# The stores of q, h and the attention's result, and the transfers of the weight sums, from GpSimd's queue

## The chip, the cores and the metric

The kernel runs on one core of a Trainium2 chip, in fp32. The engines of the core work on their own instruction streams, each in order, and wait for each other by semaphores: TensorE (PE, with its weight loads PEld), VectorE (DVE), ScalarE (ACT), GpSimd (POOL) and SyncE (SP). A transfer between the chip's memory and SBUF is an instruction in the stream of the engine that issues it; what it needs must be there before it goes out, and what stands behind it on that engine waits as long. The metric is device time in microseconds, smaller is better, as the median of several runs.

## The reference

An AdaLN block: a modulated layer norm, a linear attention with 16 heads of 32, and a mixture of 8 experts of which each token takes two. B = 2 batches of N = 4096 tokens, C = 512 channels. Cut to what matters:

```python
x1 = layernorm(x) * (1 + scale1) + shift1          # scale, shift, gate from c @ wmod
q, k, v = x1 @ w_qkv.T                             # 16 heads of 32
q, k = relu(q), relu(k)
vk  = einsum('bhen,bhdn->bhed', [v, 1], k)         # sum over all tokens of a batch
att = einsum('bhed,bhdn->bhen', vk, q); att = att[:-1] / (att[-1] + EPS)
x = x + gate1 * (att @ w_proj.T + b_proj)
h = layernorm(x) * (1 + scale2) + shift2
p, idx = top_k(softmax(rms(h) @ router_logits), 2)
for e in range(8):                                 # each token with its two experts
    g = h @ gating[e]                              # two halves, 512 wide each
    y[e] = (gelu(g[0]) * g[1]) @ linear[e]
out = x + gate2 * sum over the two experts of p * y
```

## The kernel before

**Blocks and passes.** The tokens are cut into 16 blocks of 512 (`TB`), eight a batch, each of four tiles of 128. vk is a sum over a whole batch, so each batch is passed twice. The first pass (`first`) makes k and q of each block, adds k^T x to a sum (L795), and writes q to the chip's memory (`q_d`). The second pass (`merge`, `attend`, `second_norm`, `route`) reads q again, makes the attention's result, adds it to x and writes that to `out`, makes the normalised h and writes it to `h2_d` (`h_d` in the profile's rows), and sends for each token and expert a small record to the map `map_d` (16 scatters a block, L1153, on POOL). The expert stage then gathers h's rows and each unit's expert weights by index (L1421 is the helper that issues the gathers, on POOL) and adds its results into `out` by scatters (L1488, POOL).

**Order of the work.** A planner weaves these parts, and a scheduler fixes each engine's order before the run. In the profile: the first pass of batch 0 to about 396 us, then the first pass of batch 1 between the second passes of batch 0 to about 876 us, then the second passes of batch 1 between the first nine large expert units to about 1410 us, then the rest of the expert units.

**Seven products for eight.** k and q of a block are made by seven quarter products in place of eight, in the order 1, 2, 6, 7, 5, 4, 3. Products 1, 2 and 4 take quarters of the turned block `xT` as they are; 6, 7, 5 and 3 take sums of quarters. `turned_sums` (L679 to L682) makes these on POOL, four operations a block, into `xs`. In batch 0 `xs` has one buffer, so a block's sums can't begin before PE's last product of the block before; in batch 1 it has two and is made a block ahead. The expert products have the same form, and need sums of quarters of the weights: `weight_sums` (L584 to L621) makes them during the first pass of batch 0, as 24 jobs (two gate halves and one linear matrix for each of eight experts). A job loads 1 MB into a buffer `wraw` (tag `tmp`, two buffers for all of them), makes four sums in place on POOL (L617), and stores 1 MB to `wgsum_d` or `wlsum_d` (L618). Three jobs are drawn for each block. The loads (L598) and stores are SP's; a job's load is issued right behind the store of the job two ahead of it, which had the same buffer, and the first two stand in front of all.

**The stores.** q is written in four stores of 256 KB a block (L777), each right behind ACT's relu of that tile (L774), from ACT's queue; q has four tiles of buffer. ACT also makes k's relu there, and PE's k^T x (`pa`, L795) takes k. The attention's result (L974, `out<-xb`) and h (L1007, `h_d<-h`) are each written in one store of 1 MB a block, also from ACT's queue.

Of the kernel before, what the change touches and what calls it, by code (L numbers as in the profile page):

```python
# [17 lines left out]
P = 128  # L18
B, N, C = 2, 4096, 512
# [34 lines left out]
def adaln_linear_attention_moe_kernel(  # L54
# [27 lines left out]
    nc = tc.nc  # L82
# [17 lines left out]
        out=upper, in_=ones, compare_op=ALU.is_gt, fill=0.0, base=0,  # L100
# [5 lines left out]
        out=head_mask, in_=ones[:, 0:GH], compare_op=ALU.is_ge, fill=0.0, base=0,  # L106
# [3 lines left out]
        out=head_mask, in_=head_mask, compare_op=ALU.is_ge, fill=0.0, base=HD - 1,  # L110
# [53 lines left out]
    def row(tag, name, bufs, where=bk):  # L164
        return where.tile([P, C], FP, tag=tag, name=name, bufs=bufs)
# [72 lines left out]
    raw = {}  # L238
# [345 lines left out]
    def weight_sums():  # L584


        jobs = []
        for e in range(E):
            rows = slice(e * P, (e + 1) * P)
            for m in range(2):  # L590
                src = wgate[rows, m * 4 * KH * QN : (m + 1) * 4 * KH * QN]
                r0 = (2 * e + m) * P
                jobs.append((src, wgsum_d[r0 : r0 + P, :], True))
            jobs.append((wlin[rows, :], wlsum_d[rows, :], False))

        def load(n):
            raw = temp(f"wraw_{n}")
            nc.sync.dma_start(out=raw.rearrange("p q n -> p (q n)"), in_=jobs[n][0])  # L598
            return raw

        ready = [load(0), load(1)]
        yield
        for n, (_, dst, left) in enumerate(jobs):
            raw = ready.pop(0)
            a, b, c, d = (raw[:, q, :] for q in range(4))
            if left:
                steps = (
                    (c, d, c, ALU.add), (d, a, d, ALU.subtract),
                    (a, c, a, ALU.subtract), (b, b, a, ALU.subtract),
                )  # L610
            else:
                steps = (
                    (a, d, a, ALU.subtract), (d, c, d, ALU.subtract),
                    (c, c, a, ALU.subtract), (b, b, c, ALU.subtract),
                )
            for to, one, two, op in steps:
                nc.gpsimd.tensor_tensor(to, one, two, op)  # L617
            nc.sync.dma_start(out=dst, in_=raw.rearrange("p q n -> p (q n)"))  # L618
            if n + 2 < len(jobs):
                ready.append(load(n + 2))  # L620
            yield  # L621


    q_d = dram.tile([B * NBLK * P, NT * C], FP, tag="qd", name="q_d")
# [60 lines left out]
    def first(b, i, acc, ksum):  # L685
# [15 lines left out]
        def lane(m, c):  # L701

            one, two = banks_of(m, c)
            at = E if m else 0
            top, low = slice(0, QN), slice(QN, C)
            for t in (c, c + 2):
                if m:
                    out_of[m][t] = row("qo", f"q_{b}_{i}_{t}", 4, ap)
                else:
                    out_of[m][t] = row("k", f"k_{b}_{i}_{t}", 4, ap)  # L710
            upper_t, lower_t = out_of[m][c], out_of[m][c + 2]

            def product(s, to):
                f = forms[m, s]
                a = at - (AHEAD.get(s, 0) if m else 0)
                for k in range(KH):
                    nc.tensor.matmul(
                        to[:, a : a + f.shape[2]], xs[s][:, k, c * P : (c + 1) * P],
                        f[:, k, :],
                        start=(k == 0 and s in (1, 2, 7)), stop=(k == KH - 1 and s in (2, 4, 3)),  # L720

                        skip_group_check=True,
                    )

            def keep(t, cols, src, new):

                to = out_of[m][t][:, cols]
                nc.vector.scalar_tensor_tensor(
                    to, src[:, at : at + QN], mv[:, t, 1:2],
                    bias[m, b][:, cols] if new else to, ALU.mult, ALU.add,  # L730
                )

            def logits(t, src, c0, new):
                to = xl[:, tile0 + t, 0:E]
                if new:
                    nc.vector.tensor_copy(to, src[:, c0 : c0 + E])
                else:
                    nc.vector.tensor_tensor(to, src[:, c0 : c0 + E], to, ALU.add)

            behind = at + QN  # L740
            for s in ORDER:
                to = two if s in (2, 7, 4) else one
                product(s, to)
                if s == 1:
                    keep(c, top, to, True)
                    if m:
                        logits(c, to, 0, True)
                elif s == 2:
                    keep(c, top, to, False)
                    if m:  # L750
                        logits(c, to, behind, False)
                elif s == 6:
                    keep(c + 2, top, to, True)
                elif s == 7:
                    keep(c + 2, low, to, True)
                elif s == 5:
                    keep(c + 2, low, to, False)
                    if m:
                        logits(c + 2, to, behind, True)
                elif s == 4:  # L760
                    keep(c + 2, top, to, False)
                    if m:
                        logits(c + 2, to, behind, False)
                else:
                    keep(c, low, to, True)
                yield
            for t in (c + 2, c):
                r = out_of[m][t]
                if m == 0:
                    if i == 0 and c == 0 and t == 2:  # L770
                        nc.vector.tensor_scalar(ksum, r, 0.0, None, ALU.max)
                    else:
                        nc.vector.scalar_tensor_tensor(ksum, r, 0.0, ksum, ALU.max, ALU.add)
                nc.scalar.activation(r, r, AF.Relu)  # L774
                if m:
                    r0 = (b * NBLK + i) * P
                    nc.scalar.dma_start(out=q_d[r0 : r0 + P, t * C : (t + 1) * C], in_=r)  # L777

        for lanes in (
            ((0, 0), (0, 1)), ((1, 0), (1, 1))  # L780
# [115 lines left out]
    def attend(b, i, kall, gm):  # L896

        r0 = b * N + i * TB
# [65 lines left out]
        for step in range(NT + 2):  # L964
            if step < NT:
                weigh(step)
            if 1 <= step <= NT:
                turn(step - 1)
            if step >= 2:
                project(step - 2)  # L970
            if step == NT and i + 1 < NBLK:
                load_xb(b, i + 1)
            if step == NT + 1:
                nc.scalar.dma_start(  # L974
                    out=out[r0 : r0 + TB, :].rearrange("(p t) c -> p t c", t=NT), in_=xt
                )
            yield

    def second_norm(b, i):

        xt = xatt.pop((b, i))
        r0 = b * N + i * TB
        blk = b * NBLK + i
        group = group_of[blk]
        lm, var, ssq = tokens[group[0]]
        j0 = (blk - group[0]) * NT
        at = slice(j0, j0 + NT)
        nc.scalar.activation(var[:, at], var[:, at], AF.Sqrt, bias=eps_ln, scale=1.0 / C)
        nc.vector.reciprocal(var[:, at], var[:, at])
        h2 = temp(f"h2_{b}_{i}", 0)  # L990
        for step in range(NT + 2):
            if step < NT:
                j = j0 + step
                nc.vector.scalar_tensor_tensor(
                    h2[:, step, :], xt[:, step, :], lm[:, j, E : E + 1], batch_rows[CB],
                    ALU.add, ALU.mult,
                )
                nc.vector.scalar_tensor_tensor(
                    h2[:, step, :], h2[:, step, :], var[:, j : j + 1], batch_rows[SB],
                    ALU.mult, ALU.add,  # L1000
                )
                sq = row("sq", f"sq_{b}_{i}_{step}", 1)
                nc.scalar.activation(
                    sq, h2[:, step, :], AF.Square, accum_out=ssq[:, j : j + 1]
                )
            if step == NT:
                nc.scalar.dma_start(  # L1007
                    out=h2_d[r0 : r0 + TB, :].rearrange("(p t) c -> p t c", t=NT), in_=h2
                )
                if b + 1 < B and i == NBLK - 1:  # L1010
                    for n in (SB, CB):
                        batch_row(n, b + 1)
            if step == NT + 1 and blk == group[-1]:
                route(b, group, *tokens.pop(group[0]))
            yield
# [873 lines left out]
```

## Time and profile before

| what | value |
|---|---|
| median of 3 runs | 2304.97 us (2301.86 to 2310.61) |
| the profiled execution | 2372.11 us |
| its span, mean granted clock of PE | 2370.4 us, 0.981 |
| transferred, mean rate over the span | 513.29 MB, 217 GB/s |
| POOL's queue, both others (share of 16 DMA engines) | 40.1%, 20.4% and 5.5% |

The profiled execution took 67 us longer than the median of the runs. Rows of the profile name the line, the engine, the operation, the tile written and read, the count, then the busy time in us, the mean duration of one in ns, and the idle time of the engine just ahead of such instructions with what ended most of it. Timeline rows begin with the start in us and the duration; "SPq" and "ACTq" are transfer issues in SP's and ACT's queue; what stands in brackets is the idle time ahead and what ended it. "Clock" is the share of full speed that PE was granted.

### The profile page before, as it was taken

The page shows a single profiled execution, that of the slowest core. Times are in us where ns is not written, and L with a number is a line of the kernel's source. Part 1 is how long each engine was busy: PE and PEld are TensorE (multiplying, and loading weights), DVE is VectorE, ACT ScalarE, POOL GpSimd, SP SyncE. Part 2 cuts the span into 40 slices and gives each one's busy share as a digit, 9 for nine tenths or more (in the row PEclk, how much of TensorE's full clock was granted, in tenths as well). Part 3 has the DMA queues.
Part 4 walks back from the last instruction along what each step waited for, and adds up shares of the span by engine and source line. Part 5 has one row for each costly group of instructions (what it writes and reads, how often), then busy time and mean ns, then how long its engine had stood idle before and what let it go on. Part 6 is the DMA issues. An engine that isn't in the chain of part 4 may idle for free. (4 is left out here: it accounts for less than half of the span.)

```text
span 2370.4 us, 26081 instructions
## 1 busy us (share of the span) xinstructions
PE 2257.7 (95%) x9456; PEld 1702.1 (72%) x9456; DVE 1523.0 (64%) x3251; ACT 535.0 (23%) x976; POOL 963.2 (41%) x840
## 2 busy tenths in 40 slices
PE   8999989999988999989998889999999999999997
PEld 4576657777766758878887767777777777777775
DVE  4866647786977756767876765555555555555554
ACT  1121212232323302333333411111111111111110
POOL 1266663003223242343535356444444444544432
PEclk9999999999999999999999989999999999999999
DMA  7688886444544444647684557777777777777774
GB/s 271 244 310 324 333 313 230 166 152 138 178 164 110 127 160 166 215 152 239 171 256 150 162 169 241 250 249 247 249 250 250 235 237 248 244 249 256 245 222 89
DMA packets 120189, 513.29 MB, mean 217 GB/s; under 512 B 19365, under 2 KB 22181, under 8 KB 84090
## 3 DMA queue, kind: packets, MB, share of 16 engines
q0 software_dynamic: 64704, 296.79, 40.1%
q1 hardware_dynamic: 41530, 164.45, 20.4%
q10 hardware_dynamic: 13824, 50.34, 5.5%
q8 instruction: 77, 1.26, 0.2%
q14 instruction: 54, 0.44, 0.1%
HBM read 378.97 MB, written 132.55 MB: 216 GB/s over the span
## 5 line engine op out<-in xcount | busy, mean ns | idle before, releaser
L1512 PE MATMUL p_g<-xT,wg 128*128 128x256 f32 x1600 | 373.0, 380 | 0.0
L1512 PEld LDWEIGHTS p_g<-xT,wg 128*128 128x128 f32 x1600 | 303.4, 191 | 45.7 <-issue 5.2
L1512 PE MATMUL p_g<-xS,wg 128*128 128x256 f32 x1200 | 286.6, 381 | 14.9 <-DVE quar_l L1520 7.6
L1512 PEld LDWEIGHTS p_g<-xS,wg 128*128 128x128 f32 x1200 | 227.4, 191 | 51.2 <-issue 8.1
L946 PE MATMUL po<-gm,qT 128*128 128x265 f32 (+1 forms) x1024 | 247.2, 391 | 4.6 <-issue 2.6
L795 PE MATMUL pa<-k,xh 128*128 128x512 f32 x512 | 234.2, 611 | 16.4 <-ACT k L774 16.3
L946 PEld LDWEIGHTS po<-gm,qT 128*128 128x128 f32 x1024 | 194.3, 194 | 40.2 <-issue 5.5
L1488 POOL DMA_INDIRECT out<-y_b,mp x100 | 162.7, 1627 | 129.2 <-DVE y_b L1485 101.2
L1153 POOL DMA_INDIRECT map_d<-pair,slot x128 | 133.5, 1043 | 176.0 <-DVE slot L1150 138.4
L1705 PE MATMUL pgs<-wgs,xTs 128*128 128x512 f32 x464 | 203.9, 592 | 0.0
L1512 PE MATMUL p_l<-wl,aT 128*128 128x256 f32 x800 | 193.7, 380 | 2.6 <-DVE part_l L1520 2.6
L795 PEld LDWEIGHTS pa<-k,xh 128*128 128x128 f32 x512 | 99.0, 196 | 134.4 <-issue 108.1
L617 POOL TENSOR_TENSOR wraw<-wraw 128x512 f32<-128x512 f32 x96 | 135.7, 1417 | 88.9 <-DMA wraw<-in_wgate 36.0
L1705 PEld LDWEIGHTS pgs<-wgs,xTs 128*128 128x128 f32 x464 | 88.2, 190 | 110.5 <-issue 109.5
L1512 PEld LDWEIGHTS p_l<-wl,aT 128*128 128x128 f32 x800 | 148.8, 191 | 23.6 <-DVE part_l L1520 3.0
L1512 PE MATMUL p_l<-wl,aS 128*128 128x256 f32 x600 | 144.0, 383 | 0.6 <-DVE aS L1622 0.6
L679 POOL TENSOR_TENSOR xs<-xT 128x512 f32<-128x512 f32 x16 | 21.3, 1330 | 292.1 <-DMA xT<-in_xturned 173.1
L1520 DVE TENSOR_TENSOR quar_g<-part_g,p_g 128x512 f32<-128x512 f32 x150 | 102.5, 684 | 51.1 <-PE p_g L1512 46.5
L1611 ACT ACTIVATE ge<-quar_g 128x512 f32<-128x512 f32 x100 | 63.0, 630 | 312.2 <-DVE quar_g L1520 300.9
L1512 PEld LDWEIGHTS p_l<-wl,aS 128*128 128x128 f32 x600 | 114.3, 192 | 17.9 <-issue 1.4
L1421 POOL DMA_INDIRECT xg_b<-h_d,mp x100 | 100.9, 1009 | 64.1 <-issue 32.5
L1520 DVE TENSOR_TENSOR part_g<-part_g,p_g 128x512 f32<-128x512 f32 x100 | 68.5, 686 | 83.8 <-PE p_g L1512 78.8
(343 smaller groups left out, 3734.7 us busy)
## 6 DMA issues: line engine op xcount, KB each, us to landing
xT<-in_xturned SPq DMA_DIRECT2D x16, 1024.0 KB
x<-in_x SPq DMA_DIRECT2D x16, 1024.0 KB
q_d<-q ACTq DMA_DIRECT2D x64, 256.0 KB
xb_d<-x SPq DMA_DIRECT2D x16, 1024.0 KB
qi<-q_d SPq DMA_DIRECT2D x64, 256.0 KB
wraw<-in_wgate SPq DMA_DIRECT2D x16, 1024.0 KB
wgsum_d<-wraw SPq DMA_DIRECT2D x16, 1024.0 KB
xb<-xb_d SPq DMA_DIRECT2D x16, 1024.0 KB
```

What stands on the lines that cost most here:

```text
L617: nc.gpsimd.tensor_tensor(to, one, two, op)
L679: nc.gpsimd.tensor_tensor(s7, x00, x10, ALU.subtract)
L795: nc.tensor.matmul(pa, xh[t][:, g * P : (g + 1) * P], ks[t], start=(t == 0), stop=(t == NT - 1),)
L946: nc.tensor.matmul(po[:, C // 2 - EX + c0 : C // 2 - EX + c1], qT[:, g * P : (g + 1) * P], gm[:, g, c0:c1], start=(g == 0), stop=(g == KC ...
L1153: ins = nc.gpsimd.indirect_dma_start(out=map_d, out_offset=IndirectOffsetOnAxis(ap=slot[:, k, t : t + 1], axis=0), in_=pair[:, k, t, :], i ...
L1421: return nc.gpsimd.indirect_dma_start(out=dst, out_offset=None, in_=src, in_offset=IndirectOffsetOnAxis(ap=ids, axis=0))
L1488: ins = nc.gpsimd.indirect_dma_start(out=out[0:N, :] if early else out, out_offset=IndirectOffsetOnAxis(ap=token(mp, t), axis=0), in_=y, i ...
L1512: nc.tensor.matmul(bank[:, c, :], left(s, c, k), rhs[:, k, :], start=(k == 0), stop=(k == KH - 1),)
L1520: nc.vector.tensor_tensor(r, one, two, ALU.add)
L1611: nc.scalar.activation(ge, g, AF.Gelu_apprx_tanh)
L1705: nc.tensor.matmul(p, xT[:, k, :], wg[:, :, quarters[k // KH], k % KH, :], start=(k == 0), stop=(k == KC - 1),)
```

## The change

In `weight_sums` loads and stores go out from GpSimd's queue. Only the first load stands in front; the load for job n+1 is written just ahead of the sums of job n, and the load behind the store is gone. The stores of q, of the attention's result and of h go out from GpSimd's queue too. That is 144 transfers (24 loads, 24 stores of sums, 64 of q, 16 of the result, 16 of h); their sizes, buffers and the sums themselves are as before. Where an instruction stands in POOL's final order is the scheduler's choice.

```diff
 def load(n):
     raw = temp(f"wraw_{n}")
-    nc.sync.dma_start(out=raw.rearrange("p q n -> p (q n)"), in_=jobs[n][0])
+    nc.gpsimd.dma_start(out=raw.rearrange("p q n -> p (q n)"), in_=jobs[n][0])
     return raw

-ready = [load(0), load(1)]
+ready = [load(0)]
 yield
 for n, (_, dst, left) in enumerate(jobs):
+
+    if n + 1 < len(jobs):
+        ready.append(load(n + 1))
     raw = ready.pop(0)
...
     for to, one, two, op in steps:
         nc.gpsimd.tensor_tensor(to, one, two, op)
-    nc.sync.dma_start(out=dst, in_=raw.rearrange("p q n -> p (q n)"))
-    if n + 2 < len(jobs):
-        ready.append(load(n + 2))
+    nc.gpsimd.dma_start(out=dst, in_=raw.rearrange("p q n -> p (q n)"))
     yield
...
-                    nc.scalar.dma_start(out=q_d[r0 : r0 + P, t * C : (t + 1) * C], in_=r)
+                    nc.gpsimd.dma_start(out=q_d[r0 : r0 + P, t * C : (t + 1) * C], in_=r)
...
-                nc.scalar.dma_start(
+                nc.gpsimd.dma_start(
                     out=out[r0 : r0 + TB, :].rearrange("(p t) c -> p t c", t=NT), in_=xt
                 )
...
-                nc.scalar.dma_start(
+                nc.gpsimd.dma_start(
                     out=h2_d[r0 : r0 + TB, :].rearrange("(p t) c -> p t c", t=NT), in_=h2
                 )
```

## The prediction

> **What bounds the kernel now.** I read the busy table first, then the same figures cut by stage, then the engines' timelines around the moved instructions.
>
> ```profile
> PE 2257.7 (95%) x9456; PEld 1702.1 (72%) x9456; DVE 1523.0 (64%) x3251; ACT 535.0 (23%) x976; POOL 963.2 (41%) x840
> ...
> L617 POOL TENSOR_TENSOR wraw<-wraw 128x512 f32<-128x512 f32 x96 | 135.7, 1417 | 88.9 <-DMA wraw<-in_wgate 36.0
> L1153 POOL DMA_INDIRECT map_d<-pair,slot x128 | 133.5, 1043 | 176.0 <-DVE slot L1150 138.4
> ```
>
> PE has work for 95% of the span, so the change can give only what PE now waits, and can take as much as it makes PE wait. POOL's 41% is a mean; by stages (window, length, then PE, PEld, DVE, ACT, POOL busy with counts, clock, DMA share, GB/s) it is not even:
>
> ```profile
> 106.00:396.00 290.00, 275.35 (x1011) 191.22 (x1010) 181.50 (x403) 56.21 (x91) 174.80 (x128) 0.98 0.85 318
> 396.00:876.00 480.00, 457.06 (x1876) 341.08 (x1875) 364.52 (x942) 142.80 (x287) 121.91 (x109) 0.98 0.44 141
> 1410.00:2371.00 961.00, 945.47 (x3912) 701.38 (x3911) 520.39 (x864) 150.30 (x263) 436.84 (x380) 0.99 0.75 236
> ```
>
> From 106 to 396 us, batch 0's first pass, POOL is busy 60% and the DMA engines 85%, at 318 GB/s. Here POOL makes both the weight sums (L617) and the sums xs of each turned block (L679 to L682), which PE needs 3.5 us after a block's start. From 1410 us on nothing the change touches is left. The timelines show the two places where a moved instruction holds PE now:
>
> ```profile
> 331.90 0.61 ACT L774 ACTIVATE q<-q 128x512 f32<-128x512 f32 x1
> 339.43 0.34 ACTq L777 DMA_DIRECT2D q_d<-q  x1
> 339.81 0.63 ACT L774 ACTIVATE k<-k 128x512 f32<-128x512 f32 x1 [7.29 <-DMA wlsum_d<-wraw]
> ...
> 340.49 15.10 PE L795 MATMUL pa<-k,xh 128*128 128x512 f32 x28 [6.87 <-ACT k L774]
> ...
> 768.48 3.78 PE L795 MATMUL pa<-k,xh 128*128 128x512 f32 x4 [8.39 <-ACT k L774]
> ```
>
> ACT has q ready at 332.5 but its store is not issued until 339.4 (it waits for a transfer), the next relu of k stands behind it, and PE behind that. At 758 to 766 us the same happens.
>
> **What the change takes away.** 96 issues leave ACT (64 of q, 16 of the result, 16 of h) and 48 leave SP. At 0.33 us that is 32 us of ACT, which is 77% idle: nothing by itself. By the Trainium skill ("DMA: Bandwidth & Descriptors", section "Issuing engines are not separate DMA queues") another issuing engine saves only the time to start a transfer, so the gain would be 0. The rows above weigh against it: the wait at the issue is the price. The first stall costs PE 6.87 us, and the 28 products after it took 15.10 us where 28 took 12.28 us at 213.7 us, 2.8 more: 9.7 us. The second costs 8.39 us and 14 products after it took 8.44 us, against 6.1 at that pace: 10.7 us. I take both as gone, **−20.4 us**; what is late next at these places is DVE's q (3.7 us of ACT's wait at 757.5), already inside PE's pace. Other waits of PE of this kind sum to under 1 us.
>
> SP's queue gets free of `SPq L618 <- POOL wraw` (115 us) and of the loads' waits behind it (37 us). SP then issues x and xT earlier. Their issue costs no PE wait now, so: nothing.
>
> **What it adds on POOL in batch 0.** Each of the 24 jobs before had its load two ahead on SP. These rows show one:
>
> ```profile
> 175.15 0.33 SPq L618 DMA_DIRECT2D wlsum_d<-wraw  x1
> 179.87 0.33 SPq L598 DMA_DIRECT2D wraw<-in_wgate  x1
> ...
> 180.34 1.27 POOL L679 TENSOR_TENSOR xs<-xT 128x512 f32<-128x512 f32 x1
> ...
> 186.87 5.31 POOL L617 TENSOR_TENSOR wraw<-wraw 128x512 f32<-128x512 f32 x4 [1.23 <-DMA wraw<-in_wgate]
> ```
>
> The store at 175.15 has landed 4.7 us later, when the load into the same buffer goes out; it lands 7.0 us after its issue, while POOL makes a block's xs. In the changed kernel there are still two buffers, so load n+1 waits for store n−1, and it stands in POOL's own order among job n's instructions. The scheduler's static order of the changed kernel puts it on average after 2.94 of job n's four sums' worth of work (47 over 16 jobs). Job n+1's sums then wait for it to land. So a job takes a load's latency plus what stands ahead of the next load; nothing of POOL's own is between except the xs steps.
>
> Latency: 7.0 us under load, 5.0 us with little in flight (358.64 to 363.64 us), plus 0.6 for POOL's own issue (0.95 us against SP's 0.33): 5.6 to 7.6 us, **taken 6.6**, as this stage is at 85% of the DMA engines. Sums: 5.31/4 and a gap each, 1.38 us. A job: 6.6 + 2.94 × 1.38 = **10.7 us**. It took 10.2 before (16.3 jobs from xs of block 2 at 132.70 to xs of block 6 at 298.27 us), but that had xs and all else inside.
>
> Between the same two points the new order has 16.7 jobs: 178 us; xs steps not under a load, about 8 × 1.38 = 11; q stores ahead of loads, about 8 × 1.26 = 10 (an indirect DMA on POOL is 1.04 us and its gap 0.2). Sum 199 us, against four blocks of 39.7 us, 159. So POOL falls **40 us** behind PE, where it had 2 to 7 us in hand before. Walking down POOL's order block by block with these prices, xs is late by 12 us at block 3, 17 at block 4 (five jobs before it), 2 at block 5 and 8 at block 6; then the jobs are used up. That is 39. Inside xs itself the third sum (L681) stands behind the first sum of a job whose load was just issued, so the latency stands inside PE's wait. The same walk with latency 5.5 gives 26 us, with 7 gives 44 and with 8 gives 56.
>
> **What hides the rest.**
> - The q stores wait on ACT's relu and block POOL behind them. In batch 0 that is in the walk; in batch 1 xs is a block ahead (slack 65 to 85 us). q's four buffers are free 28 to 40 us before reuse; the 16 map scatters ahead of some stores take 16 × 1.27 = 20 us. Hidden; without that cover up to 10 us a block.
> - The stores of the result and of h: their tiles have 30 to 40 us. In the stage from 876 to 1410 us 16 to 20 of them add 20 us to a POOL with 213 us of work in 534. One store of h stands ahead of a gather of wg, which goes some 12 us later with 30 in hand. At the stage's start four q stores stand before the gathers of xg: 2.5 us with 5 to 8 in hand. Taken as 0, bound 0 to 15.
> - 144 issues themselves: 0.95 to 1.27 us each. The Trainium skill ("SBUF — State Buffer", section "A bandwidth-pool intuition that's wrong (but worth ruling out)") speaks against the change: a transfer from GpSimd's queue took about 620 ns alone but about 3100 beside a copy on DVE, as the descriptors wait for a shared port. By the rule 144 × 2.5 = 360 us of POOL, and 30 us more in the walk's 12 or so exposed issues. The trace: 128 scatters into map_d, beside a DVE busy 76% of that stage, mean 1043 ns. I go by the row.
>
> **Sum.** 39 − 20.4 = +19 us. On the profiled execution, 2372.1 us, 2391 us. The median shown is 67 us (2.9%) below that execution; the waits are transfers and do not scale with it, so 2305 + 19 = **2324 us**.
>
> **Rivals.**
> 1. *Faster: the ACT stalls outweigh.* Place: the loads of wraw in batch 0. Price: the latency of one; below 5.0 us PE's loss falls under the 20.4 us gained (the walk gives 22 us at 5.0, 16 at 4.0), and a queue of SP's that waits for nothing could remove part of the other waits: PE idles 14.7 us from 106 to 396, of which I counted 6.9, and 22.9 from 396 to 876, of which 8.4. Half of the rest is 11. For it: 5.0 us at 358 us, and the median is 67 us shorter than this execution. Against: that load had the queues to itself. 16 − 20.4 − 11 = −15, 2290; with less of it, 2300.
> 2. *Nothing measurable.* Latency near 5.5 and one stall returning elsewhere: +26 − 20 = +6, 2300 to 2316. For it: DMA share 0.85 is high, not full. Against: five jobs stand ahead of block 4's xs whatever the latency.
> 3. *POOL is much worse.* Issues at 1.63 us (the row of the scatters out<-y_b), latency 8 or more, a gather of weights held behind a store: 56 + 12 × 0.7 + 15 − 20 = +59, 2364. For it: 318 GB/s already, and a store and a load now contend from one queue. Against: SP's transfers leave the other queue empty.
>
> That the change does not do what it says is out: the order shows 144 issues on POOL and none of these on ACT or SP.
>
> **Chances.** Likeliest case (+12 to +40) 0.50, rival 1 0.15, rival 2 0.23, rival 3 0.12. About 0.5% (11.5 us) is what a measurement of this kernel can tell from no change, so faster is below 2293, slower above 2316.5. Two thirds of rival 1 lie below, the rest and all of rival 2 between: faster 0.10, same 0.28, slower 0.62. The likeliest case's own range is 2315 to 2345; the range with a part of rivals 2 and 3 is 2297 to 2360.
>
> **What would show it.** Right: PE waits of 10 us or so before the product with xs at blocks 3, 4 and 6 of batch 0, released by POOL's last two steps of xs; POOL waiting for the load of wraw 6 to 7 us a job; the two waits at `pa <- k` gone; the end of batch 0's pass at about 396 + 29 us. Wrong: POOL's waits for wraw under 4 us, PE's blocks still 39.7 us long in batch 0; PE waits in the stage after 876 us released by POOL's gathers; POOL's new issues over 2 us each beside DVE.

## The result: 2.4% slower, and the profile after

| | us |
|---|---|
| changed kernel, median of 4 runs | 2362.0 (2356.3 to 2365.3) |
| kernel before beside it, median of 4 runs | 2303.4 (2300.5 to 2310.6) |
| ratio, 95% interval | 1.0247 (1.0215 to 1.0279) |
| forecast | 2324, range 2297 to 2360 |

The loss is 58 us, three times the 19 that were forecast. Here is the page of the changed kernel (the busy times and three of its groups: busy us and mean ns, then the idle time ahead and what ended it):

```profile
PE 2250.7 (96%) x9456; PEld 1706.3 (72%) x9456; DVE 1523.9 (65%) x3251; ACT 533.9 (23%) x975; POOL 1037.5 (44%) x984
...
L796 PE MATMUL pa<-k,xh 128*128 128x512 f32 x512 | 227.6, 598 | 0.3 <-ACT k L775 0.3
...
L620 POOL TENSOR_TENSOR wraw<-wraw 128x512 f32<-128x512 f32 x96 | 131.5, 1371 | 90.4 <-DMA wraw<-in_wgate 43.8
...
L778 POOL DMA_DIRECT2D q_d<-q x64 | 35.6, 557 | 235.4 <-ACT q L775 235.4
```

The busy shares of the engines tell little: PE even has a larger one. What is to be seen is in the idle columns. PE's wait for ACT's k is gone (0.3 us), a plain transfer costs POOL 0.56 us, and POOL now stands for 235 us at stores of q (none of it in the first pass of batch 0). The list of waits of the same kernel (us in total, times, longest) has what is new:

```profile
DVE h L995 <- DMA h_d<-h: 45.9, 6, 15.3
POOL wraw L620 <- DMA wraw<-in_wgate: 43.8, 15, 8.4
POOL wraw L620 <- DMA wraw<-in_wlin: 43.0, 8, 8.5
...
PE p0one L718 <- POOL xs L682: 35.9, 5, 13.6
```

POOL waits for the landing of nearly every load of weights, 3.8 us each, and PE waits 35.9 us for POOL's xs, which it did not do before. The longest of these waits, in POOL's timeline (start, duration) and then in PE's:

```profile
246.02 0.56 POOL L598 DMA_DIRECT2D wraw<-in_wlin  x1
...
248.36 0.54 POOL L621 DMA_DIRECT2D wgsum_d<-wraw  x1
252.50 1.26 POOL L620 TENSOR_TENSOR wraw<-wraw 128x512 f32<-128x512 f32 x1 [3.59 <-DMA wraw<-in_wlin]
253.72 1.25 POOL L680 TENSOR_TENSOR xs<-xT 128x512 f32<-128x512 f32 x1
...
258.58 0.56 POOL L598 DMA_DIRECT2D wraw<-in_wgate  x1
...
260.38 1.26 POOL L682 TENSOR_TENSOR xs<-xT 128x512 f32<-128x512 f32 x1
```

```profile
247.05 1.05 PE L718 MATMUL p1two<-q,xT 128*128 128x264 f32 x4
261.70 2.08 PE L718 MATMUL p0one<-k,xs 128*128 128x256 f32 x4 [13.59 <-POOL xs L682]
...
267.19 1.03 PE L718 MATMUL p0one<-k,xT 128*128 128x256 f32 x4
```

xs of this block can't start until a sum in front of it has its load, and that load was issued only at 246.02. When PE goes on, its first four products take 2.08 us instead of 1.03.

### The profile page after: what moved, and what is told of

Same layout as the page of the kernel before. It is cut to its first block, busy times and chain, and to the rows that moved or that the text cites. A ratio compares the mean times of both kernels' runs of the same rounds, so it can differ in the third digit from the quotient of the medians.

```text
span 2354.5 us, 26084 instructions
## 1 busy us (share of the span) xinstructions
PE 2250.7 (96%) x9456; PEld 1706.3 (72%) x9456; DVE 1523.9 (65%) x3251; ACT 533.9 (23%) x975; POOL 1037.5 (44%) x984
## 5 line engine op out<-in xcount | busy, mean ns | idle before, releaser
L1513 PEld LDWEIGHTS p_g<-xS,wg 128*128 128x128 f32 x1200 | 228.9, 192 | 39.9 <-issue 4.3
L947 PE MATMUL po<-gm,qT 128*128 128x265 f32 (+1 forms) x1024 | 239.8, 383 | 1.0 <-ACT qT L939 0.7
L796 PE MATMUL pa<-k,xh 128*128 128x512 f32 x512 | 227.6, 598 | 0.3 <-ACT k L775 0.3
L1513 PEld LDWEIGHTS p_l<-wl,aT 128*128 128x128 f32 x800 | 149.0, 191 | 20.4 <-issue 2.2
L778 POOL DMA_DIRECT2D q_d<-q x64 | 35.6, 557 | 235.4 <-ACT q L775 235.4
L1714 DVE TENSOR_TENSOR ar<-pgs,ges 128x512 f32<-128x512 f32 x29 | 20.1, 692 | 150.7 <-PE pgs L1706 145.3
```

Of the source, the lines that this page charges most:

```text
L778: nc.gpsimd.dma_start(out=q_d[r0 : r0 + P, t * C : (t + 1) * C], in_=r)
L796: nc.tensor.matmul(pa, xh[t][:, g * P : (g + 1) * P], ks[t], start=(t == 0), stop=(t == NT - 1),)
L947: nc.tensor.matmul(po[:, C // 2 - EX + c0 : C // 2 - EX + c1], qT[:, g * P : (g + 1) * P], gm[:, g, c0:c1], start=(g == 0), stop=(g == KC ...
L1513: nc.tensor.matmul(bank[:, c, :], left(s, c, k), rhs[:, k, :], start=(k == 0), stop=(k == KH - 1),)
```

## The experiments

Chips differ: the kernel before had a median of 2305 us on the chips of e9 to e15, 2356 on that of e1 to e4 and 2377 on that of e5 to e8. So each ratio is to runs of before on the same chip, and profiles are set side by side where their chips' times of before agree; where they don't, the text says so. The length of a block in the first pass of batch 0, below, is from one end of its last product `pa` to the next.

**e1, the kernel before once more.** No edit. The profile that the forecast read took 67 us longer than the median, so the first question was whether its waits are to be had at all.

> The kernel before, unchanged, profiled a second time: the profile that the prediction used took 67 us longer than the median. Theory A (the two waits of ACT at q's store, 6.9 and 8.4 us of PE, belonged to that one execution): this profile is near 2305 us, PE has no gap over 4 us at pa behind ACT's k, the first pass of batch 0 ends near 386 us. Theory B (they are in every execution): both gaps are here again, the pass ends near 396 us.

This execution took 2363.7 us, on a chip where that is normal (2356.4). The pass ended at 388.7 us, and PE's waits at pa were:

```profile
PE pa L795 <- issue: 4.0, 1, 4.0
PE pa L795 <- ACT k L774: 3.5, 7, 1.4
```

3.5 us behind ACT's k in place of 16.3; the gap of 6.87 us is not there, and what is left of the other is 4.0. On the two gaps theory A holds; its time near 2305 us did not come, and need not on this chip. The stages tell where the 67 us of the forecast's profile lie. From the last `pa` of batch 0 to that of batch 1 it took 479.9 us, e1 473.8 and e10 (below, a chip at 2305) 450.2; from there to the last product `po` of batch 1, 454.2, 460.1 and 421.7. So 62 us of its distance to e10 lie in these two stages, and it runs there like a chip such as e1's; the two gaps are a small part. On which chip it ran is not on record.

**e2, e3 and e4, parts of the change alone.**

```diff
 # e2: as the change, but
-    nc.gpsimd.dma_start(out=q_d ...)   # and out, h2_d
+    nc.scalar.dma_start(out=q_d ...)
 # e3: as before, but
-    nc.scalar.dma_start(out=q_d ...)   # and out, h2_d
+    nc.gpsimd.dma_start(out=q_d ...)
 # e4: as before, but
-    nc.sync.dma_start(out=dst, in_=raw ...)
+    nc.gpsimd.dma_start(out=dst, in_=raw ...)
```

> Only the weight sums' loads and stores go from GpSimd's queue, as in the change; q, the result and h stay on ACT. Theory A (the loads wait in POOL's own order and make xs late): the four PE gaps before the products with xs stay, the first pass loses about 40 us, time about 2345. Theory C (the q stores in POOL's order hold the sums): the gaps go, time under 2320.

> Only the stores of q, of the result and of h go from GpSimd's queue; the weight sums stay on SP as before. Theory A: no PE gap at xs over 3 us, time 2303 to 2320, the part above 2303 being what the change costs outside the first pass. Theory C: over 2335.

> Only the stores of the weight sums go from GpSimd's queue; the loads stay on SP two ahead. The bytes on GpSimd's queue are half those of the change's sums. Theory A (what costs is that POOL itself waits for a load): 2300 to 2312, no PE gap at xs. Theory D (transfers from GpSimd's queue are slower or disturb the others): about half of the change's loss, 2325 or more.

e2: 1.0269 (1.0239 to 1.0299), with five PE waits for xs of 4.6 to 17.7 us, 61 in all. e3: 1.0021 (1.0007 to 1.0035), but with one PE wait at xs of 8.4 us that theory A did not expect. So on this chip the weight sums carry nearly all of the loss. e4 fell out against theory A: 1.0238 (1.0209 to 1.0267), though POOL waits directly for no transfer that it issued. (It waits 82 us for SP's loads, and these wait for the stores.) It also has the two gaps of the forecast's kind again, 8.6 and 9.0 us of PE behind a store of q on ACT:

```profile
297.79 0.61 ACT L774 ACTIVATE q<-q 128x512 f32<-128x512 f32 x1
308.30 0.33 ACTq L777 DMA_DIRECT2D q_d<-q  x1
308.67 0.63 ACT L774 ACTIVATE k<-k 128x512 f32<-128x512 f32 x1 [10.26 <-DMA wraw<-in_wgate]
...
309.35 14.50 PE L795 MATMUL pa<-k,xh 128*128 128x512 f32 x28 [9.04 <-ACT k L774]
```

So such gaps are not of one execution alone; how often they come is not known. The order on POOL tells why e4 proves less than it seems: the scheduler, given stores on POOL, put 22, 23 and 24 sums between the xs of blocks 2 to 5, where before had 20, 14 and 14 and the change 15, 19 and 15. The edit was one line, the kernel that came out was another. From here on a kernel is read by the sums between two xs as well.

**e5, the changed kernel once more; e6, its transfers of weights back on SP; e7, fewer jobs ahead of xs; e8, loads two ahead.**

```diff
 # e6: as the change, but (load n+1 still just ahead of the sums of job n)
-    nc.gpsimd.dma_start(out=raw ...)   # and the store to dst
+    nc.sync.dma_start(out=raw ...)
 # e7: as the change, but a job's first sum gets an order behind the last xs step
+    tc.add_manual_dep(ins, xs_done[0].name, ... NoSync ...)
-    elif n and done in (0, SEVEN, 2 * SEVEN):
+    elif n and done in (0, SEVEN):
 # e8: as the change, but
-    raw = temp(f"wraw_{n}")
+    raw = temp(f"wraw_{n}", 0 if n % 3 == 2 else None)
-    ready = [load(0)]
+    ready = [load(0), load(1)]
-    if n + 1 < len(jobs): ready.append(load(n + 1))
+    if n + 2 < len(jobs): ready.append(load(n + 2))
```

> The changed kernel, unchanged, profiled beside this chip's runs of the kernel before, so that the two can be set side by side stage by stage. If the whole loss is in the first pass of batch 0: that pass ends about 40 us later than the 388.7 us of the repeated profile of before, plus products at a lower clock behind each wait, and the later stages take as long as there (474 us for the second, 592 for the third), within 10 us. If the stores of q, of the result and of h cost in the second or third stage, these are longer by more than 10 us.

> The change with one thing undone: loads and stores of the weight sums go from SP again, but as in the change one load in front and load n+1 written just ahead of the sums of job n. POOL makes 16 sums between two blocks' xs (15, 19, 15, 16 in the changed kernel). Theory A (POOL itself waits for loads and stores in its order): 2.4% of loss falls to 0 to 0.5%. Theory E (the depth of one load, or where the scheduler puts the sums, whatever the queue): 1.5% or more stays.

> The changed kernel with its sums held back: the sums of a job stand behind the xs of the block in which they are drawn, and two jobs are drawn per block in place of three (the rest in batch 1). Between the xs of blocks 3 to 7 stand 2 to 2.5 jobs in place of 4. Theory A and E (PE waits because more jobs stand ahead of xs than 40 us hold at 11 to 12 us each): 2 x 12 + 10 is under 40 us, so only the wait at blocks 2 and 3 stays: loss 0.5 to 1%. Theory D (transfers of GpSimd's queue disturb the others): 2% or more stays.

> The changed kernel with a third buffer for the raw weights (one that the first pass leaves unused) and loads two jobs ahead, all from GpSimd's queue still. Six jobs stand ahead of the xs of block 2 here (3 in the change), then 3.5 to 4.3 a block as before. Theory A (the load's latency is exposed in POOL's order, 10.7 us a job): POOL's waits for wraw fall under 2 us a job, a job takes about 8 us, one PE wait of 10 to 15 us stays at block 2 and none after it: loss 0.7 to 1.2%. Theory F (the transfers themselves cannot go faster than 11 us a job): POOL waits as long as in the change, PE waits 30 us at block 2 and again after: loss 2.4% or more.

| kernel | ratio (95%) | blocks 1 to 7 of the first pass, us | sum |
|---|---|---|---|
| e5, the change | one run | 40.6, 49.7, 48.6, 55.0, 44.2, 47.8, 39.1 | 325 |
| e6, weights on SP | 0.9955 (0.9926 to 0.9985) | 40.5, 38.6, 39.4, 39.2, 39.9, 38.5, 39.5 | 276 |
| e7, two jobs a block | 1.0018 (1.0003 to 1.0033) | 40.4, 49.6, 47.6, 40.4, 38.4, 38.5, 38.5 | 293 |
| e8, two ahead | 1.0143 (1.0110 to 1.0177) | 40.2, 72.0, 38.7, 46.3, 54.1, 51.5, 38.4 | 341 |

e5 took 2398.1 us, only 0.9% above this chip's runs of before. Against e1 its first pass ended 45.6 us later, at 434.3 us, and the second and third stage were not longer, 463.9 and 588.2 us against 474 and 592. As far as two chips can be set against each other, the loss here lies in the first pass alone.

e6 is the cleanest of them: with the weights' queue changed and an even 16 sums between two xs, the pass is 49 us shorter than in e5. A depth of one load is not the cause, nor is the order alone: the kernel before has 20 sums ahead of the xs of block 3 and no wait there, the change 15 and a wait of 6.0 us. That POOL issues the weights' loads and stores is the cause. In e5 from job 3 to job 19 a job took 12.3 us, in e6 10.1. e7 agrees, though by its own expectation it does not tell order from queue: with 2 to 2.5 jobs ahead of xs the blocks are at 38.5 us, and only the waits at blocks 2 and 3 are left; theory D, that transfers of POOL's queue disturb the others, is out. e8 is theory A's partial miss. The waits for loads fell as expected, from 58 to 26 us between 150 and 330 us, but now POOL stood 25 us at the issue of loads, for the store whose buffer they take, and the sums of two jobs were interleaved. Six jobs ahead of block 2 made that block 72 us long. One wait had been traded for another of the same kind: an instruction on POOL that waits for a transfer, with xs behind it.

**e9 and e10, on a chip like the first; e11 and e12, loads and stores apart.**

```diff
 # e10: as before, but
-    ready = [load(0), load(1)]
+    ready = [load(0)]
+    if n + 1 < len(jobs): ready.append(load(n + 1))
-    if n + 2 < len(jobs): ready.append(load(n + 2))
 # e11: as the change, jobs held behind xs (three a block), and
-    nc.gpsimd.dma_start(out=dst, in_=raw ...)
+    nc.sync.dma_start(out=dst, in_=raw ...)
 # e12: as the change, jobs held behind xs (three a block), and
-    nc.gpsimd.dma_start(out=raw ...)
+    nc.sync.dma_start(out=raw ...)
```

> The changed kernel again, timed against the kernel before on a further chip, since its one execution beside e6 was only 0.9% above the runs of before there, while the first result was 2.47%. If the loss is a property of the two programs: 1.9 to 2.7%. If it depends on the chip (before's own first pass being longer on some chips): 0.7 to 1.5%.

> The kernel before with one edit: one load in front and load n+1 written just ahead of the sums of job n; every transfer stays where it was (SP and ACT). POOL makes an even 16 sums between two blocks' xs (20, 14, 14, 16, 20 before). If e6's gain of 0.45% came from this spacing: 0.3 to 0.8% faster. If it came from ACT's being rid of its stores: within 0.2% of before, or slower.

> The change with the stores of the weight sums back on SP and only the loads on GpSimd's queue, the sums of a job held behind the xs of the block in which they are drawn: 16, 12, 12, 12 sums between the xs of blocks 3 to 7. Theory A, in the form that the wait for the load is what costs: POOL waits for stores of SP at the load's issue and for the load at the sums; a job takes 10 us or more, blocks 5 to 7 of the first pass are 2 to 8 us longer than 39.4. In the form that the stores cost: these blocks take 39 to 40 us.

> The same with the other half: the loads on SP, one ahead, the stores of the weight sums on GpSimd's queue, with the same 16, 12, 12, 12 sums between the xs of blocks 3 to 7. POOL never waits for a transfer of its own here, only for loads from SP. Theory A: blocks 5 to 7 of the first pass take 39 to 40 us. If a store from GpSimd's queue, landing about 10 us after its issue against 5 to 6 from SP, holds the next load into its buffer: a job takes 11 us and these blocks are 2 to 6 us longer.

e9: 1.0237 (1.0216 to 1.0259), the first result again. e10: 0.9999 (0.9988 to 1.0010), so it stands for before on this chip, and the two can be read by stage. The windows are cut at each kernel's own stage ends (window, length, PE, PEld, DVE, ACT, POOL busy with counts, clock, DMA share, GB/s); e9, the changed kernel:

```profile
106.00:426.60 320.60, 279.01 (x1009) 195.97 (x1008) 183.07 (x402) 56.31 (x91) 206.22 (x200) 0.94 0.77 285
426.60:881.10 454.50, 447.85 (x1876) 337.73 (x1875) 362.48 (x941) 143.10 (x287) 153.05 (x158) 1.00 0.47 150
881.10:1442.70 561.60, 535.27 (x2573) 457.14 (x2572) 421.83 (x944) 177.37 (x327) 254.62 (x239) 0.98 0.66 207
1442.70:2352.00 909.30, 892.72 (x3680) 658.84 (x3678) 490.14 (x815) 140.85 (x246) 404.77 (x349) 0.99 0.75 233
```

and e10, which times as before does:

```profile
106.00:389.40 283.40, 274.29 (x1012) 190.69 (x1011) 182.75 (x404) 56.02 (x91) 171.79 (x128) 0.99 0.88 328
389.40:839.60 450.20, 447.48 (x1876) 337.63 (x1875) 363.25 (x941) 142.92 (x287) 122.70 (x108) 1.00 0.48 151
839.60:1391.90 552.30, 533.80 (x2573) 457.21 (x2572) 421.82 (x944) 178.36 (x328) 246.35 (x220) 0.98 0.66 208
1391.90:2298.00 906.10, 892.72 (x3680) 658.58 (x3678) 489.95 (x815) 140.88 (x246) 405.15 (x349) 0.99 0.75 234
```

Of 54 us between the two executions, 37.2 arise in the first pass, 4.3 in the second stage, 9.3 in the third and about 3 in the last. In the first pass the DMA engines are busy for a smaller share in the changed kernel (0.77 against 0.88, at 285 against 328 GB/s): it is not their capacity that makes the pass longer.

e11 and e12 did not tell apart what they were made for. They have the same 12 sums between the xs of blocks 4 to 7, and there PE waits for xs in neither: 12 sums are few enough for both. Blocks 5 to 7 take 42.6, 41.2 and 44.0 us in e11 and 40.6, 40.8 and 39.9 in e12, but the extra time in e11 is in waits of PE for DVE and ACT, not for POOL. The blocks ahead of these say more. With 16 sums ahead of it, block 4 waits 14.3 us for xs in e11; in e12, with 15, not at all, and its one wait in batch 0, 22.0 us at block 3, stands behind 21 sums, as in e4. POOL's waits in e11, at the issue of loads (L600) and at the sums (L622):

```profile
POOL wraw L600 <- DMA wgsum_d<-wraw: 38.5, 11, 6.4
POOL wraw L622 <- DMA wraw<-in_wgate: 34.4, 7, 8.3
POOL wraw L622 <- DMA wraw<-in_wlin: 22.9, 6, 6.9
POOL wraw L600 <- DMA wlsum_d<-wraw: 18.9, 4, 5.9
```

57 us of these are at the issue, which in e12 SP bears, but there POOL waits longer at the sums (99 us). Block 4 points to the loads: 16 sums ahead of it cost no wait in e6 and e10, with the loads on SP. But e11 and e12 are single executions, and their held-back order is of their own. So that loads and stores together make the loss is shown; that the loads alone do, or how it divides, is not. Both runs, of 2375.5 and 2348.0 us, also have a PE wait at batch 1's start, 18.3 and 13.1 us, for an xs behind held-back jobs.

**e13, e14 and e15, the rest of the loss, and what freeing ACT is worth.** Third-stage windows pointed to the store of h. In e9, POOL's timeline:

```profile
1054.56 0.96 POOL L1154 DMA_INDIRECT map_d<-pair,slot  x1 [0.30 <-issue]
...
1086.50 0.95 POOL L1422 DMA_INDIRECT xg_b<-h_d,mp  x1 [0.30 <-issue]
1087.43 0.61 POOL L1008 DMA_DIRECT2D h_d<-h  x1
```

and DVE's, then PE's, of the same kernel:

```profile
1053.34 0.74 DVE L999 SCALAR_TENSOR_TENSOR h<-h,var,row 128x512 f32<-128x512 f32 x1
...
1079.63 0.69 DVE L1521 TENSOR_TENSOR quar_g<-m_g,p_g 128x512 f32<-128x512 f32 x1 [0.96 <-PE p_g L1513]
1095.80 1.42 DVE L995 SCALAR_TENSOR_TENSOR h<-xb,lm,row 128x512 f32<-128x512 f32 x2 [15.48 <-DMA h_d<-h]
1097.13 0.68 DVE L1521 TENSOR_TENSOR quar_g<-part_g,p_g 128x512 f32<-128x512 f32 x1
```

```profile
1097.87 2.50 PE L1513 MATMUL p_g<-xT,wg 128*128 128x256 f32 x5 [7.40 <-DVE quar_g L1521]
```

DVE has h whole at 1054.1, but its store went out 33 us later, behind 23 indirect transfers of POOL at some 1.4 us each: the last twelve of 16 scatters into the map (which come for two blocks at a time), then eleven gathers and scatters of the expert stage. The expectation below counted seven of them. The tile of h has one buffer, so DVE waits for the store to land before it makes the next h; the sum that PE needs is behind that h on DVE.

```diff
 # e13: as the change, but
-    nc.gpsimd.dma_start(out=h2_d ...)
+    nc.scalar.dma_start(out=h2_d ...)
 # e14: as e6
 # e15: as e6, but the stores to out and h2_d on nc.scalar
```

> The changed kernel with the stores of h alone back on ACT. In the changed kernel one store of h stands behind seven indirect DMAs in POOL's order at 1087 us, the next h has the same single buffer, DVE waits 15.5 us for the store to land and PE 7.4 us behind DVE. If this is the third stage's share of the loss: that gap of PE goes, DVE's wait for h_d<-h in that stage falls from 29 us to 12 or less, the third stage is 6 to 10 us shorter, and the loss goes from 2.4% to 2.0 or 2.1%. If the gap has another cause, it stays and the loss is 2.3% or more.

> The kernel of e6 again (weight sums on SP, one load ahead; stores of q, of the result and of h on GpSimd's queue) on another chip, since e6 was 0.45% faster than before on its chip and the store of h should cost it some us. If e6's gain is real on every chip: 0.2 to 0.7% faster. If it was that chip's (where before varied by 26 us): within 0.2% of before, or slower.

> The same with the stores of the result and of h back on ACT, so that only the stores of q go from GpSimd's queue, and the sums' loads are one ahead on SP. If moving q's stores frees PE of ACT's waits (the 20 us of the prediction): 0.3% or more faster than before. If those waits belonged to single executions: within 0.2% of before.

e13: 1.0154 (1.0140 to 1.0169). Moving this store of every block back is worth more than expected, 0.8% or about 19 us against e9. Its windows:

```profile
433.40:882.00 448.60, 447.33 (x1876) 337.62 (x1875) 364.08 (x941) 143.11 (x287) 145.05 (x146) 1.00 0.49 149
882.00:1433.00 551.00, 532.46 (x2572) 455.05 (x2572) 423.39 (x944) 177.57 (x327) 251.83 (x231) 0.99 0.67 210
```

The third stage is 10.6 us shorter than e9's and the second 5.9, both now as long as in e10; in the third stage DVE waits 2.4 us for h's store in place of 29, and the gap of PE is gone. What remains of the loss lies in the first pass, which ends at 433.4 us, with the same order of sums as in e9.

The other traces confirm the third stage, but only on the chips at 2305 us. From the last `pa` to the last `po` of batch 1 the three executions with h on ACT (e10, e13, e15) take 421.6 to 421.7 us, and the five with h on POOL (the first profile of the change, e9, e11, e12, e14) 431.0 to 434.4. On the chips of e1 to e8 both kinds lie between 451.7 and 460.1 us; there the store of h is as late, but in e5 and e6 DVE waits at most 7.6 us for it and the gap of PE is not there, and e3, with all three stores on POOL and the gap, lost 0.2% in all. So the 19 us are no constant of the change.

e14: 1.0067 (1.0054 to 1.0080). e15: 1.0014 (1.0005 to 1.0022). Freeing ACT of q's stores gains nothing, although PE's wait for ACT's k at pa falls from 5.7 us (e10) to 0.5 (e15). In e6, e14 and e15 a PE wait of about 5 us stands in its place at the first product with xs of batch 1. And e6's gain of 0.45% did not come again in e14, the same kernel on another chip. The gap of 7.5 us behind the store of h, which e14 has and e6 has not, may be a part of that difference of 1.1%. No version was found that is faster than before wherever it ran. Why e6 was faster on its chip, where before's own runs spread over 26 us, stays open.

## Why the forecast was wrong, point by point

- **"xs is late by 12 us at block 3, 17 at block 4, 2 at block 5 and 8 at block 6 … That is 39."** Right in kind and in sum. PE waited 8.6 us at block 2, 6.0 at block 3, 13.6 at block 4 and 7.5 at block 6, together 35.6. That the sum came so close is in part luck, since the wait at block 2 was not forecast and the one at block 3 was half as long. The pace of the jobs was right: one took 11.9 us (sums of job 3 begin at 158.0, of job 19 at 348.4), and the forecast's 199 us for 16.7 jobs, with xs and the stores of q, are 11.9 as well. A load landed 6.3 us after its issue in the median, where 6.6 were taken. The sign "POOL waiting for the load 6 to 7 us a job" was too high: 3.8, since some sums stand behind the issue and cover part of the landing. Under 4 us had even been named as a sign of being wrong, which it was not.
- **"I take both as gone, −20.4 us."** This step failed: it set a gain of 20 us against the loss, and the runs show none. The waits went, but most executions had not had them at that size. With q's stores on ACT they come to 4.0 and 3.5 us in e1, 5.7 in e10 and 1.9 in e2; only e4 has two of 8.6 and 9.0 us. And e15, which removes them, takes as long as e10 (1.0014 against 0.9999), with a new wait of 5.3 us for xs. The forecast had noted that its execution was 67 us longer than the median and then took that for a plain offset. That difference should have been a doubt of each stall of several us that occurs once. When such gaps come stays open.
- **"The stores of the result and of h: … Taken as 0, bound 0 to 15."** The second step that failed, on the chips at 2305 us. "Their tiles have 30 to 40 us" left out that the store may stand behind 23 indirect transfers, which take 33 us, and then needs some 8 to land. e13 shows 19 us by ratio, 16.5 of them in the windows of the second and third stage; the 10.6 of the third are confirmed by other runs, the 5.9 of the second are not (e15, with h on ACT, has 457.8 us there, e14 457.2). The forecast had looked for gathers held behind a store of h; it was a store of h held behind gathers.
- **Products behind a wait** were counted on the gain's side (2.8 and 2.3 us) and put at nothing on the loss's. In e9's first pass PE is busy 279.0 us for 1009 instructions, 4.7 us more than in e10 for 1012, at a granted clock of 0.94 against 0.99.
- **Issue costs and the shared port.** The forecast went by the trace and not by the 3100 ns beside a copy on DVE that the Trainium skill has ("SBUF — State Buffer", section "A bandwidth-pool intuition that's wrong (but worth ruling out)"). Right: the stores of q took POOL 557 ns in the mean and 771 ns at most, less than the 0.95 us of the indirect transfers.
- **Sum.** Leaving the gain out gives 39; with 5 for slow products and 16 for h it is 60, against 58 measured in the first result and 54 in e9. These terms were put together after the result, so that they meet it is no test. Rival 3 gave 2364 for other reasons (issues of 1.63 us, a latency of 8); neither was found, so that its number is close is chance.

## What to carry to other kernels

A transfer moves with its waits: on an engine that computes in order, ask what stands behind its issue, and what stands in front of it when its buffer is needed again. The loads and stores of 1 MB cost nothing that could be measured on SP, which had only transfers in its queue, and some 37 us of the first pass on POOL, which PE was waiting for. A gain read from one execution that is longer than the median has to be found in a second one before it is counted, and where a scheduler sets the order, a kernel with one line changed is to be read by its order before its time.

## What the runs showed of the hardware, not expected

- A wait costs PE more than its length. After the 13.6 us wait the same four products took 2.08 us instead of 1.03. The Trainium skill ("TensorE: Matmul & The Clock Gate", section "Part 1: The HAM clock gate (the "warmup" mystery)") has a half-rate clock after idling; the trace agrees with the factor of two, and over the first pass it shows as 4.7 us.
- A store of 1 MB from POOL's queue let the next load into its buffer go after 9.6 to 11.9 us in several jobs of e4 in a row, against 4.8 us in the clean cases from SP (e1), yet after 4.2 to 4.9 us in other jobs of e4 and e12. The packets of e4 show when: of 15 stores that POOL issued within 3.1 us of a load on SP, 13 had their first packet only 3.6 to 5.2 us after the issue; of the other nine, seven had it within 1.3 us. So the slow stores are those that come right behind a load. No run moved the store away from the load, so the cause is not shown.
- The same program's median differed by 3% between chips, and the same edit (e6, e14) gave ratios of 0.9955 and 1.0067 on two of them.
